# Selective scan with FFN: the first token's state of every second group built on GpSimd and placed by ScalarE

## The chip, the cores and the metric

The kernel runs on one core of a Trainium2 chip. The metric is device time in microseconds of one execution; the kernel before takes 2858.14 us (median of 3 runs, 2857.44 to 2862.17). All data are fp32.

## The reference

The input is x of 2 sequences, 1024 tokens each, 512 channels. One block of a state-space layer with post-layernorm, then a gated FFN of hidden size 2048 with a second layernorm:

```python
delta, B_ssm, C_ssm = split(xn @ x_proj_w.T)          # xn: gated RMS-normed x
delta = softplus(delta @ dt_proj_w.T + dt_proj_b)      # [2, 1024, 512]
A = -exp(A_log)                                        # [512, 128]
def step(h, inp):                                      # h: [2, 512, 128]
    dt, bt, ct, xt = inp
    h = exp(dt[:, :, None] * A) * h + (dt * xt)[:, :, None] * bt[:, None, :]
    y = einsum('bdn,bn->bd', h, ct)
    return h, y
x = layernorm(x + (y + x * D_param) @ out_proj_w.T)
x = layernorm(x + ffn(x))                              # silu(x@Wg.T) * (x@Wu.T) @ Wd.T
```

So each token updates a state of 512 channels by 128 state elements: a decay exp(dt A) times the old state, plus (dt x) B. The output y is the state's product with C.

## The kernel before

**Tiling of the scan.** The 128 state elements lie on the partitions. Tokens are cut into steps `st` of 32 tokens: 32 steps a sequence, 64 in all. A step has two halves `i` of 256 channels, a half has eight groups `r` of 32 channels, so there are 1024 groups `k`, 16 to a step. In each half the groups come in pairs: `pair` is 0 for even k and 1 for odd k.

**One group.** TensorE (PE) spreads (dt x) B into the PSUM tile `bu`, 32 channels by 32 tokens, with two matmuls (line 702), one for each 16 channels, and in between makes dt times A of the *next* group k+1 in two PSUM tiles `a` (line 408). ScalarE (ACT) turns each `a` into exp(-a) in `a_sb` (line 415). VectorE (DVE) runs one scan along the 1024 columns (line 722), state = a_sb * state + bu, which gives the states of all 32 tokens of 32 channels in the tile `h`. Every fp32 matmul is two passes in the trace, so a group shows four instructions of line 702 and four of line 408, and all eight run side by side on different rows of the array.

**Where the state of the step before comes in.** Column 0 of every channel in `a_sb` is zero, so the scan restarts at each channel. What the first token inherits is added before the scan: exp(dt0 A) times the last state of the step before lies in the tile `cd` (128 by 512), and VectorE adds the 32 values of the group to column 0 of each channel in `bu` (line 721), in place in PSUM. The first step of each sequence inherits nothing and has no such addition: 62 steps of 16 groups make 992 additions. `cd` is loaded by a DMA of dt0 on SyncE's queue (line 345, in `load`, emitted at group 0 of the step before), multiplied by A on GpSimd (POOL) (line 353, `carry_a`, at group 5), exponentiated on ScalarE (line 358, `carry_exp`, at group 7) and multiplied by the last states on GpSimd (line 366, `carry_h`, once for each half, at group 1 of the half after the one whose states it reads).

**Buffers.** `bu` has two PSUM tiles, so the matmuls of group k wait for the scan of group k-2. `a` has two as well, one for each half of a group, so the `a` matmuls for group k+1 wait for the exps of group k. `a_sb` has three.

**Order.** The order on each engine is written out by hand, in one loop over k (lines 679 to 750): the `bu` and `a` matmuls, the two exps of group k+1, one stage of other engines' work (`work.others`), the addition, the scan, then matmuls that fill PE until the next group. The fillers are the y matmuls of the half before (line 427: 24, 24 and 16 instructions at r = 1, 4 and 7) and, at r = 0, 2, 3, 5 and 6, up to four pieces of the other matmul work: projections for the next lot of 256 tokens (`pre`), output projection (`post`) and FFN (`ffn`) of earlier tokens. All this other matmul work goes through one PSUM tile. What FFN work is left when the scans end is done in a tail. Weights for the FFN (`w`, five buffers) are loaded on SyncE's queue, in which all DMAs of the kernel stand, in the order in which the loop emits them.

Of the kernel before, what the change touches and what calls it, by code (L numbers as in the profile page):

```python
# [9 lines left out]
FP = mybir.dt.float32  # L10
AF = mybir.ActivationFunctionType
ALU = mybir.AluOpType
# [3 lines left out]
P = 128  # L16
# [18 lines left out]
def kernel(  # L35
# [17 lines left out]
    nc = tc.nc  # L53
# [11 lines left out]
    NSB = L // S  # L65
# [15 lines left out]
    ub_d = dram.tile([NS, 4, S, 2, P], FP, name="ub_d")  # L81
# [38 lines left out]
    step_pool = tc.alloc_tile_pool(name="step", bufs=2)  # L120
# [206 lines left out]
    def toks(st):  # L327
        first = st * S - lots[lot_of[st]][0]
        return slice(first, first + S)

    prepared, carried, dus, ddts, hs, ys = {}, {}, {}, {}, {}, {}

    def load(st):


        ub = step_pool.tile([P, 2, P], FP, tag="ub", name=f"ub_{st}")
        nc.sync.dma_start(ub, ub_d[st].rearrange("g t b c -> (g t) b c"))
        prepared[st] = ub
        nc.gpsimd.tensor_copy(
            cz[st % 3][:, 28:284].rearrange("p (b w) -> p b w", w=32)[:, :, 0:4],  # L340
            made[lot_of[st]][1][:, toks(st)].rearrange("p (b t) -> p b t", t=4),
        )
        if st % NSB:
            cd = step_pool.tile([P, D], FP, tag="cd", name=f"cd_{st}")
            nc.sync.dma_start(cd, dt0_d[st : st + 1, :].to_broadcast([P, D]))
            carried[st] = cd

    def carry_a(st):

        if st % NSB == 0:  # L350
            return
        cd = carried[st]
        nc.gpsimd.tensor_tensor(cd, a_n, cd, ALU.mult)

    def carry_exp(st):
        if st % NSB:
            cd = carried[st]
            nc.scalar.activation(cd, cd, AF.Exp, scale=-1.0)

    def carry_h(st, i):  # L360

        if st % NSB == 0:
            return
        cd = carried[st].rearrange("p (b i e) -> p b i e", i=2, e=16)[:, :, i, :]
        last = hs[2 * (st - 1) + i][:, :, S - 1].rearrange("p (b e) -> p b e", e=16)
        nc.gpsimd.tensor_tensor(cd, cd, last, ALU.mult)  # L366

    def diag(j, part):

        h, a = j // 2, 2 * (j % 2)  # L370
        if h >= 2 * NS:
            return
        st, i = divmod(h, 2)
        name, m = divmod(part, 2)
        shape = [P, 2, 16, S]
        if name == 0:
            if m == 0:
                ddts[j] = half_pool.tile(shape, FP, tag="ddt", name=f"ddt_{j}")
            nc.gpsimd.tensor_tensor(  # L379
                ddts[j][:, m, :, :],  # L380
                made[lot_of[st]][0][:, a + m, toks(st)].unsqueeze(1).to_broadcast([P, 16, S]),
                hot[:, ts(i, 16)].unsqueeze(2).to_broadcast([P, 16, S]),
                ALU.mult,
            )
        else:
            if m == 0:
                dus[j] = half_pool.tile(shape, FP, tag="du", name=f"du_{j}")
            uv = prepared[st][:, 0, :].rearrange("p (m i e) -> p m i e", i=2, e=16)[:, :, i, :]
            nc.gpsimd.tensor_tensor(  # L389
                dus[j][:, m, :, :],  # L390
                uv[:, a + m, :].unsqueeze(2).to_broadcast([P, 16, S]),
                hot.unsqueeze(1).to_broadcast([P, 16, S]),
                ALU.mult,
            )
# [3 lines left out]
    def place(k):  # L398
        h, r = divmod(k, 8)
        m, pair = divmod(r, 2)  # L400
        return h, m, pair

    def decay_mm(k, b):

        h, m, pair = place(k)
        g = 2 * pair + b
        ps = ps_a.tile([P, 16, S], FP, tag="a", name=f"a_{k}_{b}")
        nc.tensor.matmul(  # L408
            ps, a_t[ts(g, 32), m, :], ddts[k // 4][ts(g, 32), m % 2, :, :],
            start=True, stop=True,  # L410
        )
        return ps

    def decay_exp(k, b, ps):
        nc.scalar.activation(  # L415
            a_sb[:, k % 3, ts(b, 16), 1:], ps[:, :, 1:], AF.Exp, scale=-1.0
        )

    def y_round(h, b):


        st, i = divmod(h, 2)
        if i == 0 and b == 0:
            ys[st] = ps_y.tile([P, 512], FP, tag="y", name=f"y_{st}")
        at = 28 + 28 * b
        for m in range(NM):
            nc.tensor.matmul(  # L427
                ys[st][ts(m, 32), ts(i, 256)], cz[st % 3][:, at : at + 32],
                hs[h][:, ts(m, 64), ts(b, 4)],
                start=(i == 0 and b == 0), stop=(i == 1 and b == 7),  # L430
                skip_group_check=True,
            )

    def y_out(st):

        tt, s = divmod(st, 4)
        if s == 0:
            yrs[tt] = post_pool.tile([P, 4, P], FP, tag="yr", name=f"yr_{tt}")
        yc = post_pool.tile([P, P, 4], FP, tag="yc", name=f"yc_{st}")
        nc.scalar.copy(yc, ys.pop(st).rearrange("p (q t) -> p q t", t=4))  # L440
        nc.gpsimd.tensor_tensor(yc, yc, pick.unsqueeze(1).to_broadcast([P, P, 4]), ALU.mult)  # L441
        nc.gpsimd.tensor_tensor(yc[:, :, 0:2], yc[:, :, 0:2], yc[:, :, 2:4], ALU.add)
        nc.gpsimd.tensor_tensor(yrs[tt][:, s, :], yc[:, :, 0], yc[:, :, 1], ALU.add)
        if s == 3:
            work.add(post(tt), front=True)
# [233 lines left out]
    for k in range(NG):  # L679
        h, m, pair = place(k)  # L680
        st, i = divmod(h, 2)
        r = k % 8

        if PARTS[r]:
            work.give_back()
        if r == 0:
            hs[h] = half_pool.tile([P, 256, S], FP, tag="h", name=f"h_{h}")
            if i == 0:
                c = lot_of[st]
                if c + 1 < NC and c not in begun:  # L690
                    begun.add(c)
                    pres[c + 1] = work.add(pre(c + 1), front=True)
                if st + 1 < NS:
                    if lot_of[st + 1] > c:
                        work.finish(pres[c + 1])
                    load(st + 1)

        bu = ps_bu.tile([P, 32, S], FP, tag="bu", name=f"bu_{k}")
        nxt = []
        for b in range(2):  # L700
            g = 2 * pair + b
            nc.tensor.matmul(  # L702
                bu[:, ts(b, 16), :], prepared[st][ts(g, 32), 1, :],
                dus[k // 4][ts(g, 32), m % 2, :, :],
                start=True, stop=True,
            )
            if k + 1 < NG:
                nxt.append(decay_mm(k + 1, b))
        if nxt:
            decay_exp(k + 1, 0, nxt[0])  # L710
        if nxt:
            decay_exp(k + 1, 1, nxt[1])
        work.others()

        if r == 0 and i == 1 and st:
            y_out(st - 1)
        if st % NSB:
            left = carried[st].rearrange("p (b i e) -> p b i e", i=2, e=16)
            first = bu[:, :, 0].rearrange("p (b e) -> p b e", e=16)
            at = 4 * m + 2 * pair  # L720
            nc.vector.tensor_tensor(first, first, left[:, at : at + 2, i, :], ALU.add)  # L721
        nc.vector.tensor_tensor_scan(  # L722
            hs[h][:, ts(r, 32), :].rearrange("p q t -> p (q t)"),
            a_sb[:, k % 3, :, :].rearrange("p q t -> p (q t)"),
            bu.rearrange("p q t -> p (q t)"),
            0.0, ALU.mult, ALU.add,
        )
        if h:
            for b in ROUNDS[r]:
                y_round(h - 1, b)  # L730
        credit = min(credit + PARTS[r], 6)
        for _ in range(min(credit, 4) if PARTS[r] else 0):
            if not work.tensor():
                break
            credit -= 1

        j, r4 = divmod(k, 4)
        if r4 == 3:
            diag(j + 2, 0)
        else:  # L740
            diag(j + 1, r4 + 1)
        if r == 1:
            if i == 0 and st:
                carry_h(st, 1)
            if i == 1 and st + 1 < NS:
                carry_h(st + 1, 0)
        if r == 5 and i == 0 and st + 1 < NS:
            carry_a(st + 1)
        if r == 7 and i == 0 and st + 1 < NS:
            carry_exp(st + 1)  # L750
# [82 lines left out]
```

## Time and profile before

| | |
|---|---|
| median of the runs | 2858.14 us |
| the profiled execution: its time, its span | 2861.14 us, 2859.4 us |
| PE busy | 2741.4 us, 96% |
| DVE busy: scans of line 722, additions of line 721 | 2340.3 us, 184.4 us |
| ACT busy, POOL busy | 1549.6 us (54%), 1782.0 us (62%) |
| first scan, last scan starts | 42.7 us, 2769.0 us |
| one step of 16 groups, mean of the steps 1 to 62 | 42.7 us |

Times are of one profiled execution, from its first instruction. A group of instructions is shown with its count, its busy time, the mean duration of one in ns, and after the bar the time that its engine was idle just before it, with what ended that idle time. A row of the waits reads: engine, tile and line that waited, what it waited for, total us, times, longest. The busy time of PE is that of pipelined matmuls whose ends are modelled, so it is not by itself a proof that PE is full.

### The profile page before, as it was taken

The numbers are of one execution on the slowest core, as the hardware profiler recorded it, in microseconds if no ns is written. First come the engines' busy times: TensorE is split into PE (matmuls) and PEld (weight loads), VectorE is DVE, ScalarE is ACT, GpSimd is POOL, SyncE is SP. The second block draws the span as 40 slices with busy tenths as digits, with TensorE's granted clock in tenths as the row PEclk, the third lists the DMA queues.
The fourth block names the chain that finished last, engine by engine and source line by source line (L and its number), as shares of the span: only waits on it lengthen the run. The fifth ranks groups of instructions, "written<-read, shape, count | busy, mean of one in ns | idle before, by whom it ended". The sixth has DMA issues, their size and how long they took to land.

```text
span 2859.4 us, 57498 instructions
## 1 busy us (share of the span) xinstructions
PE 2741.4 (96%) x22728; PEld 1490.1 (52%) x22728; DVE 2530.6 (89%) x2176; ACT 1549.6 (54%) x3105; POOL 1782.0 (62%) x2016
## 2 busy tenths in 40 slices
PE   6879999999999999999999999999999999999998
PEld 4324455555545555455555555555555555555558
DVE  3999799999999999999999999999999999899970
ACT  4545456555655556655555555655565545455543
POOL 5556566666666666666566667576666666666643
PEclk7999999999999999999999999999999999999999
DMA  2001221323223231223312332222322323323336
GB/s 74 19 28 65 86 92 62 104 76 121 71 75 109 86 119 51 83 97 98 100 44 92 105 107 99 64 81 92 112 82 71 117 95 101 99 93 110 97 114 229
DMA packets 112380, 258.67 MB, mean 90 GB/s; under 512 B 11568, under 2 KB 49456, under 8 KB 112112
## 3 DMA queue, kind: packets, MB, share of 16 engines
q1 hardware_dynamic: 112112, 254.99, 27.3%
q8 instruction: 181, 2.97, 0.4%
q14 instruction: 87, 0.71, 0.1%
HBM read 242.23 MB, written 12.71 MB: 89 GB/s over the span
## 4 chain that ended last, share of the span: by engine, by line
PE 74%; DVE 18%; issue 3%; ACT 3%; POOL 2%; DMA 1%; SPq 0%; DVEq 0%; POOLq 0%; ACTq 0%
PE bu L702 27%; PE gu L543 17%; DVE h L722 16%; PE y L427 12%; PE d L565 6%; PE a L408 5%; PE sel L186 2%; PE op L474 2%; PE xp L186 1%; DVE bu L721 1%; ACT a_sb L415 1%; DMA ub_d<-uT 1%; PE b L250 1%; PE ss L203 0%; PE z L268 0%
## 5 line engine op out<-in xcount | busy, mean ns | idle before, releaser
L722 DVE TENSOR_TENSOR_SCAN h<-a_sb,bu 128x1024 f32<-128x1024 f32 x1024 | 2340.3, 2287 | 157.5 <-PE bu L702 44.1
L415 ACT ACTIVATE a_sb<-a 128x496 f32<-128x496 f32 x2048 | 1088.9, 585 | 1161.8 <-PE a L408 1021.9
L408 PE MATMUL a<-ddt,a_t 32*128 32x512 f32 x4096 | 1247.6, 645 | 2.8 <-ACT t L314 2.8
L702 PE MATMUL bu<-du,ub 32*128 32x512 f32 x4096 | 1199.7, 644 | 49.0 <-DVE h L722 31.3
L379 POOL TENSOR_TENSOR ddt<-dt,hot 128x512 f32<-128x512 f32 x512 | 534.3, 1050 | 225.2 <-PE a L408 225.2
L543 PEld LDWEIGHTS gu<-x1T,w 128*128 128x128 f32 x4096 | 480.5, 192 | 229.1 <-issue 160.1
L389 POOL TENSOR_TENSOR du<-ub,hot 128x512 f32<-128x512 f32 x512 | 535.7, 1050 | 29.5 <-PE a L408 26.0
L543 PE MATMUL gu<-x1T,w 128*128 128x128 f32 x4096 | 535.2, 283 | 10.5 <-DVE x L478 4.0
L702 PEld LDWEIGHTS bu<-du,ub 32*128 32x128 f32 x4096 | 337.7, 184 | 376.7 <-issue 201.4
L427 PE MATMUL y<-h,cz 128*32 128x256 f32 x8192 | 527.0, 386 | 1.9 <-DVE h L722 1.3
L427 PEld LDWEIGHTS y<-h,cz 128*32 128x32 f32 x8192 | 228.7, 110 | 409.4 <-issue 275.0
L408 PEld LDWEIGHTS a<-ddt,a_t 32*128 32x128 f32 x4096 | 376.8, 184 | 28.3 <-ACT a_sb L415 18.2
L565 PE MATMUL d<-w,hid 128*128 128x256 f32 x1024 | 259.2, 396 | 11.4 <-ACT t L314 4.2
L583 POOL TENSOR_SCALAR gu<-gu 128x256 f32<-128x256 f32 x128 | 108.2, 846 | 252.5 <-ACT gu L551 251.4
L721 DVE TENSOR_TENSOR bu<-bu,cd 128x32 f32<-128x32 f32 x992 | 184.4, 186 | 88.9 <-PE a L408 84.3
L565 PEld LDWEIGHTS d<-w,hid 128*128 128x128 f32 x1024 | 186.0, 192 | 129.4 <-issue 80.8
L441 POOL TENSOR_TENSOR yc<-yc,pick 128x512 f32<-128x512 f32 x64 | 66.6, 1040 | 173.5 <-ACT yc L440 173.5
L591 POOL TENSOR_TENSOR hid<-gu,e 128x256 f32<-128x256 f32 x128 | 93.1, 728 | 113.0 <-ACT e L589 111.5
L366 POOL TENSOR_TENSOR cd<-cd,h 128x256 f32<-128x256 f32 x124 | 106.5, 859 | 46.6 <-DVE h L722 46.6
L584 POOL TENSOR_TENSOR gu<-gu 128x256 f32<-128x256 f32 x128 | 93.3, 729 | 10.7
L551 ACT COPY gu<-gu 128x512 f32<-128x512 f32 x128 | 75.3, 588 | 30.1 <-PE gu L543 30.0
L571 DVE TENSOR_TENSOR x<-x,d 128x256 f32<-128x256 f32 x64 | 25.5, 398 | 72.3 <-PE d L565 72.3
(86 smaller groups left out, 1272.9 us busy)
## 6 DMA issues: line engine op xcount, KB each, us to landing
w<-in_wgu_s_dram SPq DMA_DIRECT2D x256, 512.0 KB, 3.7
w<-in_wd_s_dram SPq DMA_DIRECT2D x128, 512.0 KB, 3.6
cd<-dt_d SPq DMA_DIRECT2D x62, 256.0 KB, 4.0
ub<-ub_d SPq DMA_DIRECT2D x64, 128.0 KB, 2.0
ub_d<-bt SPq DMA_DIRECT2D x64, 64.0 KB, 1.8
ub_d<-uT SPq DMA_DIRECT2D x64, 64.0 KB, 1.8
zT<-in_x_q_dram SPq DMA_DIRECT2D x16, 256.0 KB, 3.9
x<-in_x_dram SPq DMA_DIRECT2D x16, 256.0 KB, 3.9
```

What stands on the lines that cost most here:

```text
L366: nc.gpsimd.tensor_tensor(cd, cd, last, ALU.mult)
L379: nc.gpsimd.tensor_tensor(ddts[j][:, m, :, :], made[lot_of[st]][0][:, a + m, toks(st)].unsqueeze(1).to_broadcast([P, 16, S]), hot[:, ts(i, ...
L389: nc.gpsimd.tensor_tensor(dus[j][:, m, :, :], uv[:, a + m, :].unsqueeze(2).to_broadcast([P, 16, S]), hot.unsqueeze(1).to_broadcast([P, 16, ...
L408: nc.tensor.matmul(ps, a_t[ts(g, 32), m, :], ddts[k // 4][ts(g, 32), m % 2, :, :], start=True, stop=True,)
L415: nc.scalar.activation(a_sb[:, k % 3, ts(b, 16), 1:], ps[:, :, 1:], AF.Exp, scale=-1.0)
L427: nc.tensor.matmul(ys[st][ts(m, 32), ts(i, 256)], cz[st % 3][:, at : at + 32], hs[h][:, ts(m, 64), ts(b, 4)], start=(i == 0 and b == 0), s ...
L543: nc.tensor.matmul(ps[:, ts(2 * a + b, P)], w[:, a, k, :], x1T[:, k, :], start=(k == 0), stop=(k == NM - 1),)
L565: nc.tensor.matmul(ps[:, 0:HD], hid[:, f, :], w[:, f % 4, :], start=(f == 0), stop=(f == NH - 1),)
L583: nc.gpsimd.tensor_scalar_max(g, g, -80.0)
L702: nc.tensor.matmul(bu[:, ts(b, 16), :], prepared[st][ts(g, 32), 1, :], dus[k // 4][ts(g, 32), m % 2, :, :], start=True, stop=True,)
L721: nc.vector.tensor_tensor(first, first, left[:, at : at + 2, i, :], ALU.add)
L722: nc.vector.tensor_tensor_scan(hs[h][:, ts(r, 32), :].rearrange("p q t -> p (q t)"), a_sb[:, k % 3, :, :].rearrange("p q t -> p (q t)"), b ...
```

## The change

For odd k in the 62 steps that inherit a state, VectorE's addition goes. A new tile `cu` takes its place: it holds (dt x) B of the step's first token, for the channels of the odd groups, made without PE. Two DMAs load (dt x) of the token for the two channel sets, spread over the partitions, and a third loads B, one value for each partition, from the DRAM tile `ub_d`. ScalarE multiplies the two (one activation on 128 by 256, in `carry_a` at group 5), and GpSimd adds the inherited state to it (a second operation in `carry_h`, on 128 by 128, once a half). `cu` then holds the whole first-token column, and ScalarE copies its 32 values over column 0 in `bu` (128 by 32, from SBUF to PSUM). The copy stands behind the group's matmuls and, in ScalarE's order, after the exps of group k and ahead of the two exps of group k+1. The even groups keep VectorE's addition.

```diff
@@ load(st)
             nc.sync.dma_start(cd, dt0_d[st : st + 1, :].to_broadcast([P, D]))
-            carried[st] = cd
+            cu = step_pool.tile([P, 2, P], FP, tag="cu", name=f"cu_{st}")
+            for g in range(2):
+                nc.sync.dma_start(
+                    cu[:, g, :], ub_d[st, 2 + g, 0:1, 0, :].to_broadcast([P, P])
+                )
+            b0 = step_pool.tile([P, 1], FP, tag="b0", name=f"b0_{st}")
+            nc.sync.dma_start(b0, ub_d[st, 0, 0, 1, :].unsqueeze(1))
+            carried[st] = cd, cu, b0
@@ carry_a(st)
-        cd = carried[st]
+        cd, cu, b0 = carried[st]
+        nc.scalar.activation(cu, cu, AF.Copy, scale=b0)
         nc.gpsimd.tensor_tensor(cd, a_n, cd, ALU.mult)
@@ carry_h(st, i)
+        cd, cu, _ = carried[st]
+        first = cu.rearrange("p g (m i e) -> p m i g e", i=2, e=16)[:, :, i, :, :]
+        part = cd.rearrange("p (m o g i e) -> p m o i g e", m=4, o=2, i=2, e=16)[:, :, 1, i, :, :]
...
         nc.gpsimd.tensor_tensor(cd, cd, last, ALU.mult)
+        nc.gpsimd.tensor_tensor(first, first, part, ALU.add)
@@ the loop, behind the matmuls of group k and ahead of the exps of group k+1
+        if st % NSB and pair:
+            nc.scalar.copy(
+                bu[:, :, 0].rearrange("p (g e) -> p g e", e=16),
+                carried[st][1][:, :, ts(2 * m + i, 16)],
+            )
         if nxt:
             decay_exp(k + 1, 0, nxt[0])
...
-        if st % NSB:
-            left = carried[st].rearrange("p (b i e) -> p b i e", i=2, e=16)
+        if st % NSB and not pair:
+            left = carried[st][0].rearrange("p (b i e) -> p b i e", i=2, e=16)
             first = bu[:, :, 0].rearrange("p (b e) -> p b e", e=16)
             at = 4 * m + 2 * pair
             nc.vector.tensor_tensor(first, first, left[:, at : at + 2, i, :], ALU.add)
```

More of the change, by code (lines that the diff above doesn't have):

```diff
@@ L356, in carry_exp @@
         if st % NSB:
-            cd = carried[st]
+            cd = carried[st][0]
             nc.scalar.activation(cd, cd, AF.Exp, scale=-1.0)
@@ L363, in carry_h @@
             return
-        cd = carried[st].rearrange("p (b i e) -> p b i e", i=2, e=16)[:, :, i, :]
+        cd, cu, _ = carried[st]
+        first = cu.rearrange("p g (m i e) -> p m i g e", i=2, e=16)[:, :, i, :, :]
+        part = cd.rearrange("p (m o g i e) -> p m o i g e", m=4, o=2, i=2, e=16)[:, :, 1, i, :, :]
+        cd = cd.rearrange("p (b i e) -> p b i e", i=2, e=16)[:, :, i, :]
         last = hs[2 * (st - 1) + i][:, :, S - 1].rearrange("p (b e) -> p b e", e=16)
         nc.gpsimd.tensor_tensor(cd, cd, last, ALU.mult)
+        nc.gpsimd.tensor_tensor(first, first, part, ALU.add)
     def diag(j, part):
```

## The prediction

> **What bounds the kernel now.** I read the page's shares and chain first, then the waits, then the groups by shape, then one handover instruction by instruction, and last two stretches of equal work, one without any addition.
>
> ```profile
> PE 2741.4 (96%) x22728; PEld 1490.1 (52%) x22728; DVE 2530.6 (89%) x2176; ACT 1549.6 (54%) x3105; POOL 1782.0 (62%) x2016
> ...
> PE 74%; DVE 18%; issue 3%; ACT 3%; POOL 2%; DMA 1%; SPq 0%; DVEq 0%; POOLq 0%; ACTq 0%
> PE bu L702 27%; PE gu L543 17%; DVE h L722 16%; PE y L427 12%; PE d L565 6%; PE a L408 5%; PE sel L186 2%; PE op L474 2%; PE xp L186 1%; DVE bu L721 1%; ACT a_sb L415 1%; DMA ub_d<-uT 1%; PE b L250 1%; PE ss L203 0%; PE z L268 0%
> ```
>
> PE and DVE are both nearly full, but the chain of work that ended last runs on PE for 74% and on DVE for only 18%. So DVE time is worth something in about a fifth of the span. How much PE really loses to DVE is in the waits:
>
> ```profile
> ACT a_sb L415 <- PE a L408: 1021.9, 732, 5.2
> DVE bu L721 <- PE a L408: 84.3, 174, 7.9
> PE bu L702 <- DVE h L722: 31.3, 47, 1.3
> PEld a L408 <- ACT a_sb L415: 18.2, 64, 0.7
> PE bu L702 <- DVE bu L721: 14.4, 25, 1.5
> ```
>
> PE stands idle for DVE's scans 31.3 + 14.4 = 45.7 us in 72 events; DVE waits for PE in 174 of its additions. The 18.2 us are PE waiting for the exps, which matters below.
>
> Two stretches of 16 groups each, the first without one addition (first step of the second sequence), the second with 16 of them (columns: length, then busy us of PE, PEld, DVE, ACT, POOL):
>
> ```profile
> 1406.50:1449.27 42.77, 41.06 (x314) 20.29 (x313) 37.03 (x21) 24.66 (x51) 27.66 (x31) 1.00 0.22 72
> 1449.27:1491.98 42.71, 42.39 (x341) 22.04 (x340) 40.29 (x37) 26.10 (x51) 27.63 (x30) 1.00 0.19 62
> ```
>
> DVE is 3.3 us less busy without additions, and the step takes as long (42.77 against 42.71 us; the mean step is 42.70). It is one step and its PE work differs a little, but it says that in the body a lighter DVE is worth little.
>
> **What goes from DVE.** 496 additions of line 721, 186 ns each, 92 us busy. Back to back, a scan with its addition takes 1494.46 - 1491.98 = 2.48 us and one without 11.10 / 5 = 2.22 us (five scans merged in the timeline at 1404.31), so each is worth up to 0.26 us, 129 us in all, if DVE set every group. It does not. The DVE part of the chain is 16% for scans, 457 us or 200 scans; 97 of those that I count in the chain are of odd groups: 97 x 0.26 = 25 us at most. From PE's side: 72 waits, with one odd group in a typical stretch of two or three chain scans, 72 x 0.26 = 19 us. Clipped at the length of each wait it is 16 us. The low end is the stretch above: 0. I take -12. PE also stands idle for DVE's other work in the same queue (lines 465, 478, 571), some 17 us in 21 events: -3 (0 to -5).
>
> A page of the Trainium skill would have it otherwise: Perfetto Trace Analysis, "Identifying the Most-Contended Engine", says that matmul busy time is no measure of PE's distance from its roofline, that the share of LDWEIGHTS is, and that the engine with the highest occupancy is to be relieved first. By that PE is at 52%, DVE at 89% is the bound, and the change would give the whole 129 us. The equal stretches speak against it: here the row decides.
>
> **What ACT gets: 496 copies ahead of the exps.**
>
> ```profile
> L199 ACT ACTIVATE xT<-xT,vec 128x256 f32<-128x256 f32 x28 | 11.9, 499 | 0.0
> ...
> L443 POOL TENSOR_TENSOR yr<-yc 128x128 f32<-128x128 f32 x64 | 27.9, 436 | 5.0
> ...
> L608 ACT ACTIVATE rstd_a<-rstd_a 128x1 f32<-128x1 f32 x16 | 3.2, 203 | 0.5
> ...
> L244 ACT COPY low<-xp 128x256 f32<-128x256 f32 x7 | 2.6, 375 | 2.5 <-PE xp L186 2.5
> ```
>
> No row shows ACT writing PSUM. A copy of 256 takes 375 ns (line 244) and one of 512 588 ns (line 551): 0.83 ns an element, 162 ns fixed, so 189 ns for 32; from line 608 it is 203 + 26 = 229 ns. Neighbours overlap by about 0.11 us (two exps of 585 ns stand as 1.06), so a copy pushes what follows by 0.08 to 0.12 us, or 0.23 without overlap. I take 0.10. For a PSUM target ScalarE: Activation LUTs, "What ACT_TABLE_LOAD costs", gives an estimate of 186 + 0.833 x 32 - 93 = 120 ns; no run here has shown it, and by it the next term would be 14 instead of 12.
>
> For the scan itself the copy is no loss: the addition and its handover take 0.30 us from the end of the matmuls (1404.01 to 1404.31), the copy 0.19 to 0.23 and one handover of 0.06. Nor does ACT come late to it: the copy stands where the exp of k+1 stood, and that exp begins within 0.07 us of the matmuls' end in 19 of 20 odd groups. The loss is behind the copy, in PE's order:
>
> ```profile
> 1403.84 1.07 PE L427 MATMUL y<-h,cz 128*32 128x256 f32 x16
> 1403.96 1.07 ACT L415 ACTIVATE a_sb<-a 128x496 f32<-128x496 f32 x2 [1.24 <-PE a L408]
> 1404.01 0.20 DVE L721 TENSOR_TENSOR bu<-bu,cd 128x32 f32<-128x32 f32 x1
> ...
> 1404.85 0.69 PE L702 MATMUL bu<-du,ub 32*128 32x512 f32 x1
> ...
> 1405.09 0.69 PE L408 MATMUL a<-ddt,a_t 32*128 32x512 f32 x1
> ```
>
> This is r = 7. PE's filler is 16 y matmuls, 1.0 us, and then it needs the `a` tiles back. The second exp ends at 1405.03, and the second `a` matmul starts at 1405.09 instead of 1404.85: PE's set is 0.24 us longer. A copy ahead of the exps adds its full push. In the trace of before the second `a` matmul starts within 0.07 us of that exp's end behind 147 odd groups: 83 of 124 at r = 7, 39 at r = 5, 25 at r = 3, none at r = 1 (there the slack is 0.20 us). 147 x 0.10 = 14.7; a fifth of them lies where PE waits for DVE anyway: +12. Bounds: 147 x 0.8 x 0.07 = 8, and at 0.23 with r = 1 joining in 30.
>
> **What PE gets.** The two programs' orders of instructions have the same matmuls, but 494 of the `a` matmuls (first one, odd k) get a second wait, for an earlier `a` matmul of PE itself: the exp of an odd group no longer waits for PE (the copy has done so), and the ordering of the buffer is written as a wait of its own. It is always met long before. Such a wait is one more instruction in PE's queue (51 ns in the row of line 408, 245 of them before); PE's queue is mostly ahead and hides it, and the `a` matmul starts 6 ns behind its `bu`. Where the queue was empty after a wait it starts 104 ns behind. With some 40 such places, +4; bounds 0 and 494 x 0.051 = 25.
>
> **The rest.** GpSimd: 124 additions of 128x128, at 436 ns (line 443) 54 us, on an engine that is 62% busy and on the chain for 2%: +2 (0 to 15); queued behind them are the `ddt` and `du` products that PE reads three or four groups later. ACT: 62 activations of 128x256 with a column scale, 499 ns (line 199), 31 us, plus all the evacuations behind the copies 0.1 us later; ACT is on the chain for 3%: +3 (0 to 10). SyncE: 186 more DMAs of some 0.37 us to issue (as line 345), 1.1 us a step, ahead of the loads of `w`; PE's weight loads wait for `w` under 4 us in all, so +1 (0 to 5). The loads have five groups, 13 us, until `carry_a`; a landing takes 4.0 us.
>
> **Sum.** -12 - 3 + 12 + 4 + 2 + 3 + 1 = +7 us on the profiled execution's 2861.14 us, which stands 3.0 us above the median: 2861 + 7 - 3 = 2865 us.
>
> **Rivals.**
> - *DVE was the real bound* (other side, faster). Every stretch on the chain shortens by its odd additions: -25, side work -5, copies at 0.07 in 70% of the 147 places +7, the rest +3: -20, 2838 us; less pronounced, down to -6. It decides once the gain at the 72 waits passes 22 us, 0.31 us a wait. For it: 45.7 us of PE waits that DVE ends. Against it: the step without additions.
> - *The copy is dear.* At 0.23 us a copy and with PE's extra waits half exposed: +30 + 12 + 6 - 15 = +33, 2891 us. For it: no row of ACT writing PSUM, with a 128-byte stride. Against it: the 0.11 us of overlap in all ACT rows.
> - *Nothing moves.* PE's order hides both, as in the step without additions: 2858 us. Against it: r = 7, where PE waits for ACT now.
>
> **How the numbers follow.** What a measurement of this kernel can tell from no change is about 0.2%, 5.7 us. My case (net -3 to +16) 0.50, of which 0.30 is slower and 0.20 the same; DVE rival (-6 to -25) 0.27, nearly all faster; dear copy (+16 to +45) 0.18; nothing moves 0.05. So faster 0.25, same 0.27, slower 0.48. The range 2842 to 2891 cuts off the far part of both rivals, about 1 in 10 on each side. The forecast's own range is 2855 to 2874.
>
> **What would show it.** The additions at 496, DVE busy some 90 us less; copies at 0.19 to 0.23 us; PE's idle time for scans down from 45.7 to about 32 us; PE waiting for exps up from 18.2 to some 30 us, most of it at r = 7; the mean step within 0.3 us of 42.7. I am wrong if the mean step falls by 0.2 us or more, if the copy takes far longer than 0.23 us, or if the odd scans now wait for ACT.

## The result, and the profile after

The changed kernel takes 2864.88 us (median of 21 runs, 2860.16 to 2876.45); the kernel before, run beside it, 2857.72 us (21 runs, 2852.23 to 2865.37). The ratio is 1.0028 with an interval of 1.002 to 1.0036: 8 us slower, 6 to 10. The forecast was 2865 us. In what follows a ratio is turned into microseconds on 2857, and single profiled executions are only used to see where time lies, since executions of one kernel differ by up to 16 us.

The page of the changed kernel, its busy shares and its chain:

```profile
PE 2764.8 (97%) x22728; PEld 1510.8 (53%) x22728; DVE 2461.2 (86%) x1680; ACT 1629.6 (57%) x3663; POOL 1839.5 (64%) x2140
...
PE 82%; DVE 7%; ACT 4%; issue 3%; POOL 2%; DMA 1%; SPq 0%; DVEq 0%; POOLq 0%; ACTq 0%
PE bu L715 29%; PE gu L556 17%; PE y L440 14%; PE d L578 8%; PE a L421 6%; DVE h L740 6%; PE sel L186 2%; PE op L487 2%; ACT a_sb L428 1%; PE xp L186 1%; DMA ub_d<-uT 1%; PE ss L203 1%; PE b L250 1%; SPq L296 0%; PE z L268 0%
```

DVE's share of the chain went from 18% to 7%, and PE took what it left (74% to 82%). DVE was relieved, and the kernel is slower: the chain changed engines, it did not get shorter.

The groups, kept apart by shape, with the scan, the copy, the remaining additions, GpSimd's new addition and ScalarE's new product:

```profile
L740 DVE TENSOR_TENSOR_SCAN h<-a_sb,bu 128x1024 f32<-128x1024 f32 x1024 | 2326.9, 2283 | 250.8 <-ACT bu L723 131.8 <-PE bu L715 44.6 <-PE a L421 9.0
...
L723 ACT COPY bu<-cu 128x32 f32<-128x32 f32 x496 | 93.9, 189 | 601.2 <-PE a L421 521.3 <-PE bu L715 75.2 <-POOL du L402 2.3
L739 DVE TENSOR_TENSOR bu<-bu,cd 128x32 f32<-128x32 f32 x496 | 92.9, 187 | 68.8 <-PE a L421 65.1
...
L379 POOL TENSOR_TENSOR cu<-cu,cd 128x128 f32<-128x128 f32 x124 | 56.7, 457 | 9.7
...
L360 ACT ACTIVATE cu<-cu,b 128x256 f32<-128x256 f32 x62 | 31.4, 506 | 0.0
```

The copy takes 189 ns, as long as the addition that it replaces. New is the 131.8 us that DVE waits for it. The waits:

```profile
ACT bu L723 <- PE a L421: 521.3, 361, 3.3
DVE h L740 <- ACT bu L723: 131.8, 248, 1.5
...
PE bu L715 <- DVE h L740: 28.2, 54, 1.1
PEld a L421 <- ACT a_sb L428: 18.7, 72, 0.8
```

PE's idle time for scans fell to 28.2 us in 54 events. Its wait for the exps hardly rose in this row (18.2 to 18.7 us), but the work set behind r = 7 did get longer. The same place in the timeline as in the prediction (a group at r = 7, engine, line, operation):

```profile
1466.09 1.07 PE L440 MATMUL y<-h,cz 128*32 128x256 f32 x16
1466.26 0.19 ACT L723 COPY bu<-cu 128x32 f32<-128x32 f32 x1 [0.51 <-PE a L421]
1466.38 1.06 ACT L428 ACTIVATE a_sb<-a 128x496 f32<-128x496 f32 x2
1466.49 2.29 DVE L740 TENSOR_TENSOR_SCAN h<-a_sb,bu 128x1024 f32<-128x1024 f32 x1 [0.20 <-ACT bu L723]
...
1467.10 0.69 PE L421 MATMUL a<-ddt,a_t 32*128 32x512 f32 x1
...
1467.50 0.69 PE L421 MATMUL a<-ddt,a_t 32*128 32x512 f32 x1
```

The exps begin 0.12 us after the copy (124 ns in the median). The second `a` matmul starts at 1467.50, 0.40 us behind the first; before, it stood 0.24 us behind it.

For a finer picture I cut the traces of all kernels at the first `bu` matmul of each group. "Set" is the time from there to the end of the group's eight `bu` and `a` matmuls, "rest" from there to the next group. Means in ns over the groups from k = 96 on, by r:

```
             r =   0     1     2     3     4     5     6     7
set   before     1305  1224  1140  1229  1282  1160  1259  1286
set   after      1427  1217  1143  1260  1316  1182  1315  1290
rest  before     1564  1380  1628  1601  1366  1455  1522  1006
rest  after      1526  1376  1595  1574  1364  1447  1483   997
```

Each r stands for 116 such groups. The sets became 265 ns longer in sum, 116 x 0.265 = 31 us; most of it, 122 ns or 14 us, at r = 0, whose set follows the exps behind r = 7, and then at r = 6 and r = 4. The rests became 160 ns shorter, 19 us. So the body (groups 96 to 1022) lost 12.3 us: 42.82 us a step became 43.03. The profiled execution of the kernel before lost 3.4 us in this body to a low clock (1.7 us each in steps 56 and 57, see the last section), which that of the changed kernel did not, so that these two executions differ by 3.8 us and the medians by 7.2.

The first steps went the other way. By group 96 the changed kernel is 9.0 us ahead (238.0 against 247.0 us for these groups). Two stretches of 20 us there, in the kernel before (length, then busy us of PE, PEld, DVE, ACT, POOL with their counts, granted clock, DMA share, GB/s):

```profile
140.00:160.00 20.00, 16.44 (x132) 6.09 (x132) 18.61 (x17) 9.90 (x20) 11.95 (x14) 0.91 0.06 14
160.00:180.00 20.00, 15.48 (x124) 5.32 (x116) 18.61 (x17) 8.02 (x16) 9.45 (x10) 0.91 0.15 47
```

and in the changed kernel:

```profile
140.00:160.00 20.00, 15.79 (x144) 6.42 (x148) 19.59 (x13) 10.20 (x25) 15.09 (x19) 1.00 0.11 30
160.00:180.00 20.00, 15.69 (x156) 6.51 (x152) 19.59 (x14) 11.28 (x25) 9.18 (x10) 1.00 0.10 30
```

Here there is no FFN work yet for PE to fill in, and DVE sets the pace. Before, DVE runs one scan and one addition every 2.48 us, 4.96 us for a pair of groups. After, two scans stand back to back and a pair takes 4.66 us:

```profile
144.60 4.46 DVE L740 TENSOR_TENSOR_SCAN h<-a_sb,bu 128x1024 f32<-128x1024 f32 x2
148.98 0.17 DVE L739 TENSOR_TENSOR bu<-bu,cd 128x32 f32<-128x32 f32 x1
149.26 4.46 DVE L740 TENSOR_TENSOR_SCAN h<-a_sb,bu 128x1024 f32<-128x1024 f32 x2
```

Eight pairs make 37.3 us, which is the measured length of steps 2 and 3 after (37.3 us each); 8 x 4.96 = 39.7 us is less than the 41.06 us that they took before. The rest of that difference, 1.4 us a step, goes with the granted clock, which is 0.91 in the one and 1.00 in the other.

### The profile page after: what moved, and what is told of

Its sections match the earlier page's. It is cut to its first block, busy times and chain, and to the rows that moved or that the text cites. A ratio compares the mean times of both kernels' runs of the same rounds, so it can differ in the third digit from the quotient of the medians.

```text
span 2863.2 us, 58234 instructions
## 1 busy us (share of the span) xinstructions
PE 2764.8 (97%) x22728; PEld 1510.8 (53%) x22728; DVE 2461.2 (86%) x1680; ACT 1629.6 (57%) x3663; POOL 1839.5 (64%) x2140
## 4 chain that ended last, share of the span: by engine, by line
PE 82%; DVE 7%; ACT 4%; issue 3%; POOL 2%; DMA 1%; SPq 0%; DVEq 0%; POOLq 0%; ACTq 0%
PE bu L715 29%; PE gu L556 17%; PE y L440 14%; PE d L578 8%; PE a L421 6%; DVE h L740 6%; PE sel L186 2%; PE op L487 2%; ACT a_sb L428 1%; PE xp L186 1%; DMA ub_d<-uT 1%; PE ss L203 1%; PE b L250 1%; SPq L296 0%; PE z L268 0%
## 5 line engine op out<-in xcount | busy, mean ns | idle before, releaser
L740 DVE TENSOR_TENSOR_SCAN h<-a_sb,bu 128x1024 f32<-128x1024 f32 x1024 | 2326.9, 2283 | 250.8 <-ACT bu L723 131.8
L421 PE MATMUL a<-ddt,a_t 32*128 32x512 f32 x4096 | 1269.9, 644 | 2.8 <-ACT t L314 2.8
L715 PE MATMUL bu<-du,ub 32*128 32x512 f32 x4096 | 1206.9, 643 | 32.5 <-DVE h L740 28.2
L715 PEld LDWEIGHTS bu<-du,ub 32*128 32x128 f32 x4096 | 345.0, 184 | 359.1 <-issue 213.1
L723 ACT COPY bu<-cu 128x32 f32<-128x32 f32 x496 | 93.9, 189 | 601.2 <-PE a L421 521.3
L421 PEld LDWEIGHTS a<-ddt,a_t 32*128 32x128 f32 x4096 | 391.8, 184 | 36.9 <-ACT a_sb L428 18.7
L739 DVE TENSOR_TENSOR bu<-bu,cd 128x32 f32<-128x32 f32 x496 | 92.9, 187 | 68.8 <-PE a L421 65.1
```

Source lines behind the costliest of these rows:

```text
L421: nc.tensor.matmul(ps, a_t[ts(g, 32), m, :], ddts[k // 4][ts(g, 32), m % 2, :, :], start=True, stop=True,)
L715: nc.tensor.matmul(bu[:, ts(b, 16), :], prepared[st][ts(g, 32), 1, :], dus[k // 4][ts(g, 32), m % 2, :, :], start=True, stop=True,)
L723: nc.scalar.copy(bu[:, :, 0].rearrange("p (g e) -> p g e", e=16), carried[st][1][:, :, ts(2 * m + i, 16)],)
L740: nc.vector.tensor_tensor_scan(hs[h][:, ts(r, 32), :].rearrange("p q t -> p (q t)"), a_sb[:, k % 3, :, :].rearrange("p q t -> p (q t)"), b ...
```

## The experiments

All ratios are to the kernel before, run beside the edited one. "Theory 1" of the first four is the forecast's own account: a relief of DVE that the push on the exps and the preparation more than eat up.

**What the relief is worth: no addition and nothing in its place.** To the kernel before; the odd groups inherit nothing.

```diff
-        if st % NSB:
+        if st % NSB and not pair:
             left = carried[st].rearrange("p (b i e) -> p b i e", i=2, e=16)
```

> The kernel before with VectorE's addition left out in the odd groups and nothing put in its place: the odd groups' states of the step before are left out of the computation, ScalarE, GpSimd, SyncE and PE are as before. It prices the relief of VectorE alone. Theory 1 (PE sets the pace, the relief is worth the 12 + 3 us of the forecast, most of it in the first 100 groups, where PE has little filler): 12 to 22 us faster than before, about 2840. Theory 2 (VectorE is the bound and the change loses its gain because VectorE now waits for the copies): 60 us faster or more, below 2800.

Measured: 2838.24 us, ratio 0.9931 (0.9919 to 0.9943), 19.7 us faster. That DVE's additions are hidden nearly everywhere holds: 496 additions at 0.26 us would be 129 us. The relief is inside 12 to 22, but above the 15 us that the forecast booked. From the end of the `bu` matmuls to the odd scan it takes 179 ns here, 422 before and 331 in the changed kernel (medians from k = 96 on): this kernel also spares a handover that the changed kernel must pay. In its trace about half of the gain stands in steps 1 to 4 (11.3 us); the other half, some 12 us with steps 56 and 57 left out, is spread over the body, where half of the steps gain nothing and the others 0.1 to 1.1 us.

**The push alone.** To the kernel before, with all additions left on DVE: a copy of 32 columns that nobody reads, at the place of the changed kernel's copy.

```diff
+    spare = main.tile([P, S], FP, name="spare")
...
+        if st % NSB and pair and nxt:
+            nc.scalar.copy(spare, nxt[0][:, 0, :])
         if nxt:
             decay_exp(k + 1, 0, nxt[0])
```

> The kernel before with all its additions on VectorE, and in the same 496 odd groups one ScalarE copy of 32 columns of the `a` tile into a spare SBUF tile nobody reads, ahead of the two exps. It gives ScalarE's push on the exps and the extra waits in PE's order (495 of them) without any relief of VectorE and without VectorE waiting for ScalarE. Theory 1 (the push lengthens PE's set behind r = 7 by 0.12 us, less elsewhere): 10 to 18 us slower than before, about 2871, with PE's set of r = 0 longer by some 0.12 us. Theory 2 (the loss is VectorE waiting for the copy): within 3 us of before.

Measured: 2865.89 us, ratio 1.0034 (1.0022 to 1.0046), 9.7 us slower (6 to 13), at the low end of theory 1's 10 to 18. The sets grew most at r = 0 (68 ns), r = 4 (34) and r = 6 (32), behind r = 7, 3 and 5, where the prediction counted tight groups. But this copy does not push as much as that of the changed kernel. It reads PSUM and writes SBUF, where the other reads SBUF and writes PSUM; it takes about as long (186 ns), yet the exp behind it begins 82 ns after it, not 124 (medians). That fits the set at r = 0, which grew by 68 ns here and by 122 in the changed kernel. So 9.7 us is a price for a push of 82 ns; by an estimate in proportion, 124 ns would cost some 15 us.

**The preparation alone.** To the kernel before: the three DMAs, ScalarE's product and GpSimd's second addition as in the changed kernel, but no copy, and all additions on DVE.

```diff
+            nc.sync.dma_start(b0, ub_d[st, 0, 0, 1, :].unsqueeze(1))
...
+        nc.scalar.activation(cu, cu, AF.Copy, scale=b0)
...
+        nc.gpsimd.tensor_tensor(first, first, part, ALU.add)
```

> All that prepares the new tile (three DMAs a step, the product on ScalarE, the second addition on GpSimd), but no copy, and all 992 additions on VectorE as before. It prices the forecast's +2 +3 +1 = +6 us. Theory 1: 1 to 6 us slower than before. Theory 2 has the same: 0 to 6.

Measured: 2864.47 us, ratio 1.0034 (1.0021 to 1.0048), 9.7 us slower. The forecast had +6 for this.

**The changed kernel with DVE's addition kept at r = 7.**

```diff
-        if st % NSB and pair:
+        if st % NSB and pair and r != 7:
             nc.scalar.copy(
...
-        if st % NSB and not pair:
+        if st % NSB and (not pair or r == 7):
```

> The changed kernel, but the groups r = 7 keep VectorE's addition (372 copies instead of 496). Theory 1 (the loss is the push behind r = 7): PE's set of r = 0 is back at 1.31 us and the kernel 9 to 14 us faster than the changed one, at 2851 to 2856, so a little faster than before. Theory 2 (VectorE's time decides, and 124 additions come back to it): the same as the changed kernel or up to 8 us slower.

Measured: 2868.46 us, ratio 1.004 (1.0028 to 1.0052): no better than the changed kernel, which is what theory 2 said. The set at r = 0 did fall back, from 1427 to 1306 ns, as expected, and the profiled body is 4.4 us shorter than the changed kernel's. But the first 96 groups took 245.5 us instead of 238.0: 3.2 us of this are in step 0, where nothing was edited, and 4.2 us in steps 1 to 5, the ones that DVE bounds, where a quarter of the odd groups have their addition back. Here, undoing the push also undid relief. This trace also lost 6.8 us in steps 43 and 44 against the changed kernel, with a low clock in both, so a single trace does not settle how much each is worth.

**The preparation in two halves.** To the kernel before: the three DMAs alone, and ScalarE's product with GpSimd's second addition alone, on tiles that are set once.

```diff
+            cu = step_pool.tile([P, 2, P], FP, tag="cu", name=f"cu_{st}")
+            for g in range(2):
+                nc.sync.dma_start(
...
+            nc.sync.dma_start(b0, ub_d[st, 0, 0, 1, :].unsqueeze(1))
```

```diff
+            cu, b0 = cu_fix[st % 2], eps_l
...
+        nc.scalar.activation(cu, cu, AF.Copy, scale=b0)
...
+        nc.gpsimd.tensor_tensor(first, first, part, ALU.add)
```

> The kernel before with the three new DMAs a step alone (tiles that nobody reads; no product, no second addition, no copy, all additions on VectorE). Theory 3 (the preparation is dear because its DMAs stand ahead of four loads of `w` in SyncE's queue at the start of an FFN tile, and those loads issue and land late, as in the run with the whole preparation, where PE waited 8.5 us for one): 5 to 9 us slower than before, the median landing of `w` from the first weight matrix near 4.5 us instead of 3.7. Rival (the preparation's price is the added work of GpSimd and ScalarE): within 3 us of before.

> The other half of the preparation alone: the product on ScalarE and the second addition on GpSimd work on tiles that are set once, no new DMAs, no copy, all additions on VectorE. Theory 3: within 3 us of before. Rival: 5 to 9 us slower.

Measured: the DMAs alone 2863.49 us, ratio 1.0023 (1.0013 to 1.0034), +6.6 us; the work alone 2863.21 us, ratio 1.0019 (1.001 to 1.0027), +5.4 us. Together 12, against 9.7 for both at once: each half costs something, neither is hidden, and of theory 3 and its rival neither is right alone. Where it lies is seen by setting the step lengths of two traces against each other. Most steps agree to 0.05 us, and what is lost stands in a few. The work alone, against the kernel before: step 34 +2.2, step 29 +1.6 (a low clock, see the last section), steps 10, 11, 12 and 42 between +0.5 and +0.9; the changed kernel shows the same steps (34: +2.8). In step 34 the chain of the changed kernel runs through GpSimd without a gap, with the new addition in it, and from there to ScalarE and PE:

```profile
1520.07 0.84 POOL cd L378
1520.91 0.07 issue
1520.98 0.46 POOL cu L379
1521.44 1.22 POOL u L279
1522.66 1.01 POOL du L402
...
1527.45 0.43 ACT e L599
```

So the 0.46 us go in whole: from the start of `du` at 1519.06 to the start of the exp `e` the chain takes 8.39 us, and 7.85 us for the same work in the kernel of a later experiment that has the copies without their preparation. PE, which is late by then, gets a lower clock on top:

```profile
1529.52 0.69 PE L421 MATMUL a<-ddt,a_t 32*128 32x512 f32 x1
...
1531.56 1.94 PE L440 MATMUL y<-h,cz 128*32 128x256 f32 x16
...
1534.46 1.06 PE L421 MATMUL a<-ddt,a_t 32*128 32x512 f32 x1
...
1537.75 0.59 PE L421 MATMUL a<-ddt,a_t 32*128 32x512 f32 x1
```

16 y matmuls take 1.94 us instead of 1.07, an `a` matmul 1.06 instead of 0.59, for some 7 us. The granted clock of 1520 to 1540 us is 0.83 in this trace; it is 1.00 up to 1530 us and 0.50 from 1530.3 to 1537.1 us, while the kernel with the copies alone has 1.00 throughout. Half a clock for 6.8 us can cost up to 3.4 us (an estimate from these figures), so most of what step 34 loses can be the clock's and not the addition's.

The DMAs show at step 44. SyncE's queue in the changed kernel (start, duration of the issue), where a new step and a new FFN tile begin together:

```profile
1918.66 0.38 SPq L345 DMA_DIRECT2D cd<-dt_d  x1
1919.14 0.86 SPq L348 DMA_DIRECT2D cu<-ub_d  x2
1920.05 0.42 SPq L352 DMA_DIRECT2D b<-ub_d  x1
1920.51 3.75 SPq L526 DMA_DIRECT2D w<-in_wgu_s_dram  x4
```

and in the kernel before:

```profile
1915.03 0.38 SPq L345 DMA_DIRECT2D cd<-dt_d  x1
1915.47 2.13 SPq L513 DMA_DIRECT2D w<-in_wgu_s_dram  x4
```

Three more DMAs stand ahead of the four loads of `w`, and these themselves take 3.75 instead of 2.13 us to issue. In the changed kernel's chain the first of them is then what PE waits for:

```profile
1920.05 0.42 SPq L352
1920.47 0.04 issue
1920.51 7.91 DMA w<-in_wgu_s_dram
1928.42 0.14 issue
1928.56 2.02 PE gu L556 x16
```

The median time to landing of these loads went from 3.7 to 4.3 us (4.5 with the DMAs alone). This place accounts for some 2 us (step 44: +2.0 with the DMAs alone). Where the other 4 to 5 us lie that the DMAs cost in the medians stays open.

**The preparation later.** To the changed kernel: the three DMAs at group 2 instead of group 0, ScalarE's product at group 7 instead of 5.

```diff
+        if r == 2 and i == 0 and st + 1 < NS:
+            load_first(st + 1)
...
             nc.scalar.activation(cd, cd, AF.Exp, scale=-1.0)
+            nc.scalar.activation(cu, cu, AF.Copy, scale=b0)
```

> The changed kernel with the three DMAs of a step moved from group 0 to group 2 of the step before, and the product on ScalarE from group 5 to group 7, so that they stand behind the loads of `w` that begin an FFN tile. Theory 3: 4 to 8 us faster than the changed kernel, 2857 to 2861. Rival: the same as the changed kernel, 2865 plus or minus 3.

Measured: 2867.35 us, ratio 1.0033 (1.0019 to 1.0047): a miss, not better than the changed kernel. The landing at step 44 is no longer late there, but step 34 still loses 2.5 us, to the same GpSimd addition, which this edit leaves in place.

**The change in the first steps only.** To the changed kernel: copy, preparation and second addition only while st < 6, then the kernel before.

```diff
+EARLY = 6
...
-        if st % NSB and pair:
+        if st % NSB and pair and st < EARLY:
...
-        if st % NSB and not pair:
+        if st % NSB and not (pair and st < EARLY):
```

> The change in the steps 1 to 5 alone (where PE has no FFN to do), the kernel before from step 6 on. In the traces the changed kernel is 8 to 11 us ahead there and loses it later. Theory 1: 7 to 11 us faster than before, about 2848, and the fastest kernel that computes everything. If VectorE's relief is worth something all along (theory 2), it is only a tenth of it, 2 us.

Measured: 2851.34 us, ratio 0.9976 (0.9964 to 0.9989), 7 us faster than the kernel before (3 to 10) and the fastest complete kernel of the study. In its trace steps 1 to 4 are 2.7, 3.8, 3.8 and 1.6 us shorter than before, as in the changed kernel.

**The copies without their preparation.** To the changed kernel: `cu` set once to a constant, no DMAs, no product, no second addition; the odd groups inherit the constant.

```diff
-            cu = step_pool.tile([P, 2, P], FP, tag="cu", name=f"cu_{st}")
...
+            cu, b0 = cu_fix[st % 2], eps_l
...
-        nc.scalar.activation(cu, cu, AF.Copy, scale=b0)
...
-        nc.gpsimd.tensor_tensor(first, first, part, ALU.add)
```

> The changed kernel with its copies and without their preparation: two cu tiles are set once to 0.001, none of the three DMAs, no product with b, no second GpSimd addition; the copies stand where the changed kernel has them, ahead of the exps, and the even groups keep VectorE's addition. The odd groups get a constant in place of their first-token state, so that part of the computation is replaced. Known so far against the kernel before: no addition and no copy in odd groups -19.7 us, a copy's push with VectorE's additions kept +9.7, preparation without copies +9.7; these add up to 0, while the whole change costs +7 to +8. Theory 1 (the remainder belongs to the copy, because an odd scan must still wait for it where the kernel without additions had nothing to wait for): -2 us, bounds -5 to +1, about 2855; VectorE is then still waiting for ScalarE before its odd scans, some 250 times and 130 us in all. Theory 2 (the remainder is between preparation and copies, as a late cu or a late evacuation that only both together cause): -10 us, bounds -13 to -7, about 2847. Rival (the copies alone are all of the loss): +5 or more.

Measured: 2854.9 us, ratio 1.0002 (0.9992 to 1.0012): +0.6 us, -2 to +3. Theory 1. Its waits are those of the changed kernel:

```profile
DVE h L735 <- ACT bu L718: 126.1, 242, 1.7
...
PE bu L710 <- DVE h L735: 27.6, 54, 1.0
```

So a copy for an addition is an even trade on this kernel, and the loss of the change is its preparation: 8.0 - 0.6 = 7.4 us with the copies in place, 9.7 without them. In the traces it is even again: up to group 96 this kernel is as far ahead as the changed one (237.6 and 238.0 us), and the changed kernel's body is 10.2 us longer, of which step 34 has 2.4, steps 44, 27, 10 and 42 between 0.8 and 1.2 each.

**The copy behind the exps.** To the changed kernel.

```diff
+        if nxt:
+            decay_exp(k + 1, 0, nxt[0])
+        if nxt:
+            decay_exp(k + 1, 1, nxt[1])
         if st % NSB and pair:
             nc.scalar.copy(
...
-        if nxt:
-            decay_exp(k + 1, 0, nxt[0])
-        if nxt:
-            decay_exp(k + 1, 1, nxt[1])
```

> The changed kernel with one edit: the copy of an odd group stands behind the two exps of the group after it instead of ahead of them. The push on the exps and the extra self-waits of the matmuls are gone; the copy, and with it the odd scan, comes up to 1.06 us (two exps) later after its matmuls. Theory 1 (the push on the exps is the loss): 8 to 10 us below the changed kernel, about 2855, with the set of r = 7 matmuls back at the length it has in the kernel before. Theory 2 (the time from the end of the matmuls to the odd scan matters as much): slower than the changed kernel by 3 to 10 us, 2868 to 2875, with VectorE waiting for ScalarE ahead of nearly all 496 odd scans and TensorE waiting for scans well above the changed kernel's 28.2 us.

Measured: 2907.87 us, ratio 1.0179 (1.0166 to 1.0192), +51 us. Theory 2, and more than it said.

```profile
DVE h L740 <- ACT bu L727: 291.8, 349, 3.5
...
PEld bu L715 <- DVE h L740: 115.9, 116, 2.1
...
PE bu L715 <- DVE h L740: 89.2, 163, 1.3
```

The push is gone (the set at r = 0 is 1296 ns), but the odd scan now starts 1253 ns after its matmuls instead of 331, and PE waits for scans three times as long. DVE has the same operations in both kernels, so this is the price of the handover, with what the missing push gives back already taken off: 43 us against the changed kernel for 0.92 us on 496 groups, 87 ns a group. A late operand costs this kernel more than a busy engine.

**More for PE to do at r = 7.** In the changed kernel and, as its base, in the kernel before: 24 y matmuls at r = 7 and 16 at r = 4, instead of 16 and 24.

```diff
-ROUNDS = ((), (0, 1, 2), (), (), (3, 4, 5), (), (), (6, 7))
+ROUNDS = ((), (0, 1, 2), (), (), (3, 4), (), (), (5, 6, 7))
```

> The changed kernel with one table changed: of the eight rounds of y matmuls that fill in behind the groups of a step, one moves from r = 4 to r = 7 (24 y instructions at r = 7 and 16 at r = 4 instead of 16 and 24). Behind r = 7 TensorE then has some 0.5 us more to do before it needs the tiles back from the exps, more than the copy's push of 0.12 us. Compared with the kernel before under the same table, run in the same call. If the push behind r = 7 is the main loss, the gap between the two falls from +7 to +8 us to +1 or less, and the set behind r = 7 is alike in both. If the loss lies elsewhere, the gap stays at +6 to +9. Against the shipped kernels: theory 1 gives -3 to -10 us for this kernel against the changed one; the rival gives 0 or a loss, since r = 4 then has too little to fill in.

> The kernel before with the same table (16 y instructions at r = 4, 24 at r = 7), as the base for the changed kernel with that table. Theory 1 (only the copy's push makes r = 7 tight): within 3 us of the kernel before. Rival (r = 7 is tight already, as the exps of 83 of 124 such groups are waited for in its trace): 2 to 6 us faster than the kernel before. If r = 4 is left too empty: slower by 3 or more.

Measured: the changed kernel 2856.78 us, ratio 1.0002 (0.9993 to 1.0011), 7 to 8 us below the changed kernel; the kernel before 2867.02 us, ratio 1.0037 (1.0025 to 1.0049), 10.6 us slower, the third case of its forecast. The gap between the two turned from +8 to -10: in the direction of theory 1, and further than the +1 that it gave. The timeline at r = 7 in the changed kernel with this table:

```profile
1461.94 1.50 PE L440 MATMUL y<-h,cz 128*32 128x256 f32 x24
1462.11 0.19 ACT L723 COPY bu<-cu 128x32 f32<-128x32 f32 x1 [0.51 <-PE a L421]
1462.24 1.06 ACT L428 ACTIVATE a_sb<-a 128x496 f32<-128x496 f32 x2
...
1463.39 0.69 PE L421 MATMUL a<-ddt,a_t 32*128 32x512 f32 x1
```

The exps end at 1463.30, before PE is through with y, and no `a` matmul waits. The set at r = 0 fell to 1140 ns (-287) in the changed kernel and to 1149 (-156) in the other; the set at r = 5, behind the group at r = 4 that lost its filler, rose by 216 and 192 ns. So moving the filler pays only where the copy has made r = 7 dear: 131 ns more gained, 24 more lost, 107 ns, or 12 us over 116 groups. That is these two places alone; all sets and rests of the body together moved by 69 ns, 8 us of the 18 by which the gap moved. Why the kernel before loses as much as 10.6 us stays open: 3.7 us of it stand in the first 96 groups of its trace, the rest at no one place.

## Why the prediction came out right, point by point

The time is right to the microsecond, and in part by luck. The mechanism forecast, a relief of DVE that the push on the exps and the preparation more than eat up, is what the runs show; the terms are off and offset each other. Against the runs that price them, the relief was put 5 us too small, the preparation 1 to 4 us too small, the push (with PE's own waits) 1 to 6 us too large, and the odd scan's wait for the copy was put at nothing where 5 to 11 us are left for it.

- **The relief, -12 and -3.** Too small by 5 us (-19.7 with no addition and no handover), and wrong in its place. It was spread over the 72 waits of the whole span. With no addition and no copy, half of it stands in steps 1 to 4, where DVE sets every group, and half is spread thinly over the body. In the changed kernel only the first half is still to be seen, 11.9 us (2.7 + 3.8 + 3.8 + 1.6), of which steps 2 and 3 owe 1.4 us each to the granted clock; in the body the push outweighs the rest. The prediction looked at 32 steps as if they were one, and its one step without additions, which it used as the low end of 0, could not show the 0.2 us that the body gains in the mean of a step. The Trainium skill, Perfetto Trace Analysis, "Optimization Strategy", says that the most-contended engine can change between regimes of a kernel. The trace agrees: DVE 18.6 to 19.6 of 20 us busy at 140 to 180 us, PE 19.9 to 20.0 of 20 us in a stretch of the body before (2380 to 2460 us). The kernel with the change in the first steps only is the test of it.
- **The copy, 0.19 to 0.23 us, pushing 0.10.** 189 ns and 124 ns. The interval measured agrees with the estimate of 120 ns that the prediction worked out from the Trainium skill, ScalarE: Activation LUTs, "What ACT_TABLE_LOAD costs". The 82 ns of the copy from PSUM to SBUF in the run of the push alone do not agree with it.
- **The push, +12, and PE's own waits, +4.** Together +16; the push alone, with both in it, measured +9.7, but for a push of 82 ns. The prediction's own sum gives 147 x 0.8 x 0.082 = 9.6 us for that, and 14.6 us for the 124 ns of the changed kernel, so the sum holds as far as it was tried, with the push put too small and PE's waits too large. The 494 extra waits of PE on itself are in that kernel too, and the set at r = 2 grew by only 7 ns with them: they are hidden. The place, r = 7 first, was right (14 of the 31 us by which the sets grew).
- **"For the scan itself the copy is no loss."** True against the kernel before (331 against 422 ns from matmul to scan), but the prediction also listed "the odd scans now wait for ACT" as what would make it wrong, and they do: 248 of them, 131.8 us. What it missed is that this time has a price of its own, seen when the copy stands behind the exps. With the push at +9.7 to +15, relief and push leave 5 to 11 us missing to the +0.6 that the copies measure. That this is the price of the wait is argued, not shown: the run with the copy behind the exps shows that such a wait costs time, but no run prices it at this place.
- **The rest, +6.** Somewhat small: +7.4 with the copies, +9.7 (6 to 14) without. ScalarE's product and GpSimd's addition, put at +5, measured +5.4 (3 to 8), though not as a small share everywhere: they go in whole at the few places where GpSimd is on the chain. The term that was mis-sized is the DMAs, put at +1 from the 4 us that PE waits for `w`; alone they measured +6.6 (4 to 10). In step 44 they made the chain wait for a `w` that had landed in time before.
- **What would show it.** Additions 496: yes. DVE busy: -69 instead of -90, since an addition partly overlaps the scan ahead of it (by 60 ns in the mean, before) and takes less of the merged time than its 186 ns. PE's idle time for scans 28.2, predicted 32. PE waiting for exps: predicted 30 in the row that has 18.7; the row was the wrong place, since an `a` matmul that is held back while a neighbouring `bu` matmul runs is no idle time of PE, and the longer set shows it. The mean of the steps 1 to 62 is 42.72 us, 42.70 before: inside the 0.3, with the gain of the first steps and the loss of the body (+0.21 us a step) in it.
- **The rivals.** DVE as the bound (2838) would have been right for four of the 62 steps. The dear copy (2891) fell with 189 ns. "Nothing moves" is true of the copies as a whole (+0.6), but not for the reason that it gave: relief and push are both there (-19.7 and +9.7 alone), and offset each other.

## What to carry to other kernels

Cut the span into its regimes before pricing the relief of an engine: here what the change gained, all told, lay in four steps out of 64, and giving the change to those alone turned a loss of 8 us into a gain of 7. Moving an operation to an idle engine costs what it puts in front of others there, and also the preparation of its operands: a 0.46 us addition on an engine with 2% of the chain still came in full where that engine was the chain. When an operation is moved into a dependent chain, price how long its consumer waits for it, not its own duration, and then rebalance the filler work around the place that became tight, since the old balance fits the old kernel only. And see that a run meant to price one term has that term at its size: a copy of the same length pushed the exps by 82 ns here and by 124 there.

## What the runs showed of the hardware

- **The granted clock falls to half for 3.4 or 6.8 us at a time.** With FFN work not yet there, PE waits some 0.8 to 1.3 us for DVE ahead of most groups, in both kernels (144 to 152 us). Before, stretches of 20 us there have a granted clock of 0.91: it is 0.50 from 150.8 to 154.1 us and 1.00 from there to 171.0. Single matmuls show it:

```profile
150.26 0.80 PE L702 MATMUL bu<-du,ub 32*128 32x512 f32 x1 [1.34 <-DVE bu L721]
...
150.86 1.06 PE L702 MATMUL bu<-du,ub 32*128 32x512 f32 x1
```

  1.06 us where the same form takes 0.59 at full clock. With the copies the clock is 1.00 there, though PE is no busier (15.8 and 15.7 of 20 us, before 16.4 and 15.5). With the DMAs alone, and all additions on DVE, step 2 happened to run at a clock of 1.00 and took 39.7 us, which is 8 x 4.96, against 41.06 before: so of the 3.8 us that step 2 gained, 2.4 are DVE's and 1.4 the clock's. Why the clock drops in one and not in the other is not settled. The Trainium skill, TensorE: Matmul & The Clock Gate, "What's actually happening", has the clock at half speed after an idle window of about 3.4 us, in windows that run freely. By an estimate from that page one window at half speed makes a clock of 0.91 over 20 us and costs up to 1.7 us. The traces agree in this: they show rows of 0.91 and lumps of 1.6 to 1.7 us (steps 56 and 57 of the kernel before, steps 24 and 29 with the DMAs alone, step 32 in the kernel with the change in the first steps only). They do not agree in what sets it off, if an idle window is one without work: PE's longest wait in the timeline at 146 to 152 us is 1.34 us.
- **A tiny load is slow.** `b`, 0.5 KB, one value for each partition, lands in a median of 5.9 us; the `w` loads of 512 KB of line 526, in the same queue, in 4.3 us.
- **ScalarE writes 32 values into PSUM at a stride of 128 bytes** in 189 ns, and the next exp starts 124 ns after the copy's start; the scan follows 33 ns behind the copy's end where DVE waits for it.
